# Earlier opening and denser feeding of 16-head attention stages, and zero products beside their first score maxima

## The chip, the cores and the metric

The kernel runs on one core of one Trainium2 chip. The metric is the device time of one execution in microseconds; it was taken three times. Engines are named as in the profile: PE is TensorE, the matrix engine; PEld is its load of weights; DVE is VectorE; ACT is ScalarE; POOL is GpSimd; SP is SyncE, which issues DMAs. A "granted clock" of 1.00 means that TensorE ran at its full clock, 0.50 at half.

## The reference

A sequence x of 2048 tokens with 128 features runs through fourteen residual sublayers, each on the layer norm of x. Three are softmax attention with 16 heads of 8 features, four are mixtures of 8 experts that are computed densely (Moe0 and Moe3). One of each, cut to what matters:

```python
# 16-head attention (causal and with rotary embedding in layer 0, plain in layer 2,
# with a spectral filter on q and k in layer 3)
att = einsum('bhqd,bhkd->bhqk', q, k) * (1.0 / sqrt(D))      # D = 8
att = softmax(where(causal, att, NEG_BIG), axis=-1)           # causal in layer 0 only
y = einsum('bhqk,bhkd->bhqd', att, v)
x = x + y.reshape(B, T, C) @ Wp.T + bp

# mixture of 8 experts, 128 -> 512 -> 128, every expert on every token
h = relu(einsum('td,edh->teh', xt, W1) + b1)
y = einsum('teh,ehd->ted', h, W2) + b2
x = x + einsum('ted,te->td', y, gate)                         # gate: top 2 of 8 (0 or 1 in Moe3)
```

## The kernel before

x stays in SBUF as 16 tiles of 128 tokens, in four blocks of 512 tokens (`NB` 4, `BW` 512). The list `STAGES` (L2199) names the fourteen stages in order, with their numbers: CumSum 0, Moe0 1, Causal 2, Moe0 3, Mamba 4, Mla 6, Ssm 7, Moe2 9, Attn2 10, Moe2 11, Hale 12, Moe3 13, Filtered 14, Moe3 15. Causal, Attn2 and Filtered are the 16-head stages and share the class `Attn16` (L641). Moe0 and Moe3 share the class `Moe` (L340); Moe2, which stands ahead of Attn2, is another class with a pace of its own.

**Handover between stages.** `Core.run` (L71) walks through a stage's `main`, which yields between pieces of work. At every `cur.pace`-th yield it advances the `feed` of the next stage by one step (L88). `feed` (L101) waits until the current stage is `roomy`, that is, has given back enough SBUF; then it opens the next stage, whose weight loads are issued there, and runs the early work of its blocks: `NB - own` of them, three for a 16-head stage, whose fourth is done within its own main. A block starts only when the current stage has finished that block of x, and no sooner than four steps after the one before it (`apart`), so three blocks want some 17 steps. When main has ended, what is left of the feed runs at once, one step behind another. Whatever is issued to an engine's queue runs there in that order. The stages with numbers below 12 are built in a block whose order of instructions a scheduler with a simulated timeline may change; from Hale on the order is nearly the one written. Matmuls that call `in_turn` keep their order in either.

**Moe.** `open` (L347) opens pools, loads small weights and calls `weights(e)` (L365) for two experts; the others are fetched two experts ahead within the first block. Each call loads raw f32 weights W1 and W2 into tiles from a pool `moe_s` of the whole stage (`self.two`, 2 or 1 buffers for each name) and splits each into a high and a low part in fp32r (`split`, L125 to L130, the copy on ACT and the difference on DVE). `main` (L469) goes over 4 blocks, 8 experts in a block and 4 quarters of the 512 hidden features in an expert, and yields after each quarter. A quarter is `first` (L425: three matmuls, L135 to L137, then the relu on ACT or DVE and the low part on POOL or DVE, L437 to L441) and, four quarters later, `second` (L443: L448 broadcasts the gate, three matmuls for W2, and after the fourth quarter L461 `m_t` on DVE and L462, the sum `m_acc` on POOL). After the last block four quarters drain, with a yield each, and `add_T` (L156) transposes `m_acc` and adds it to x. In the last block each expert that has been used for the last time shuts its weights' pool, for the last `SHUT` = 5 of the numbering (the order of experts is reversed in odd blocks, so the first five to be done); the stage is `roomy` after the fifth. `spare` is true unless the next stage is Mamba.

**Attn16.** The early work of a block is layer norm (L246 to L255), transposes (L262), the projection to v (L727), to k (`heads`, with L694 for the bias, L135 to L137 for the matmuls, rotary embedding at L702 to L704 in Causal, and the split), and four `slot`s that spread k over the four groups of heads (L715, copied by ACT at L717). `main` (L743) does the same for q's block 0 and runs `units` (L589): 16 units, a group of four heads by a block of queries. A unit has two passes. `pass_a` (L763) forms scores (L784), two heads at a time into a pair `ps_a` of PSUM banks, adds the causal mask on the diagonal (L787) and takes the maximum along the keys on DVE (L788); `set_max` (L800) turns the maxima (L810, L812) and a DMA (L814) writes them beside q, so that pass_b's matmuls subtract them. `pass_b` (L834) forms transposed scores (L868), takes their exponential on ACT (L874) and multiplies them with v (`av`, L847) into a PSUM tile of the tag "c"; each such step is followed by four matmuls with an all-zero weight into the same tile (L851, the "zero products": `zerob` is 128 rows by 32 columns of zeros, `wide` is 128 x 512 of ones, in bf16). The tile is taken at a unit's first AV (L841). pass_a runs ahead of pass_b by a whole unit and six pairs, so a stage begins with pass_a alone.

Of the kernel before, what the change touches and what calls it, by code (L numbers as in the profile page):

```python
# [12 lines left out]
F32 = mybir.dt.float32  # L13
# [7 lines left out]
P = 128  # L21
# [5 lines left out]
FF = 512  # L27
# [312 lines left out]
class Moe(Stage):  # L340
# [1 line left out]


    pairs, lns = False, 2
    pace = 2

    def open(self):  # L347
        c, ins, pre = self.c, self.c.ins, self.pre
        self.open_ln()
        self.lag, self.lnx, self.two = (4, 2, 2) if self.spare else (3,1,1)  # L350
        m = self.m = self.pool("moe_m")
        self.wr = c.load(m, "moe_wr", (P, E), ins[pre + "Wr"])
        self.br = c.load(m, "moe_br", (P, 4, E), ins[pre + "br"].unsqueeze(0).unsqueeze(0).to_broadcast([P, 4, E]))
        self.b1 = c.load(m, "moe_b1", (P, E, 4), ins[pre + "b1T"])
        self.b2 = c.load(m, "moe_b2", (P, E), ins[pre + "b2T"])
        self.sel = c.load(m, "moe_sel", (P, E, P), ins["sel24"], dtype=BF16)
        self.gTs, self.ngT = [m.tile([P, BW], BF16, name=f"g_gT{k}") for k in range(2)], 0
        for t in self.gTs:
            c.nc.gpsimd.memset(t, 0.0)
        self.st = self.pool("moe_s")  # L360
        self.w1, self.w2, self.L, self.gT, self.acc = {}, {}, {}, {}, {}
        for e in range(2):
            self.weights(e)

    def weights(self, e):  # L365
        if e in self.w1 or e >= E:
            return
        c, ins, pre = self.c, self.c.ins, self.pre
        wp = self.pool(f"moe_w{e}")
        for w, nm, sh, src in ((self.w1, "w1", (P, FF), ins[pre + "W1"][e]), (self.w2, "w2", (P, 4, P), ins[pre + "W2"][e].rearrange("(c p) d -> p c d", p=P))):  # L370
            raw = self.st.tile(list(sh), F32, name=f"moe_{nm}_raw", bufs=self.two)
            c.nc.sync.dma_start(raw, src)
            w[e] = tuple(wp.tile(list(sh), F32R, name=f"moe_{nm}{k}") for k in "hl")
            c.split(*w[e], raw, "a", "v")

    def logits(self, b):
        c, nc = self.c, self.c.nc
# [86 lines left out]
            self.shut(f"moe_w{e}")  # L464
            self.roomy = e == E - self.SHUT

    SHUT = 5

    def main(self):  # L469
        c = self.c  # L470
# [170 lines left out]
class Attn16(Attention):  # L641
# [45 lines left out]
    def heads(self, which, b):  # L687

        c, nc, wt = self.c, self.c.nc, self.wt
        pss = []  # L690
        for nm in (which, which + "r") if self.rope else (which,):
            pp = c.ps("b")
            if nm + "b" in wt:
                nc.tensor.matmul(pp, wt[nm + "b"], c.ones2, start=True, stop=False)  # L694
            c.mm3(pp, wt[nm], self.hl[b], start=nm + "b" not in wt)
            pss.append(pp)
        src = pss[0]
        if self.rope:
            s = slice(b * BW, (b + 1) * BW)
            cos, sin = [c.load(self.pre_k, "at_" + n, (P, BW), c.ins[n][:, s], bufs=1) for n in ("cosT", "sinT")]  # L700
            src = self.pre_k.tile([P, BW], F32, name="at_r0", bufs=1)
            nc.vector.tensor_tensor(src, pss[0], cos, ALU.mult)  # L702
            nc.vector.tensor_tensor(sin, pss[1], sin, ALU.mult)
            nc.gpsimd.tensor_tensor(src, src, sin, ALU.add)  # L704
        h, l = (self.pre_k.tile([P, BW], F32R, name=f"at_{which}{k}", bufs=1) for k in "hl")
        c.split(h, l, src, "a")
        return h, l

# [33 lines left out]

    def main(self):  # L743
        self.start()
        self.wk = self.pool("at_k", 2)
        self.qhl = self.heads("q", 0)
        self.prep(0, 0)
        self.banks()
        for b in range(self.have):
            add_bias(self.c, self.bo, b)  # L750
        self.roomy = True
        yield from self.units(self.scale)

    def prep(self, g, b):
        q = self.wk.tile([P, BW], F32R, name="at_q", bufs=self.NQ)
# [6 lines left out]
    def pass_a(self, u):  # L762

        c, nc = self.c, self.c.nc
        g, b, i0, i1 = u
        q, KT = self.qb[(g, b)], self.KT[g]
        mx = self.wk.tile([P, 4, 4, 4], F32, name="at_mx")
        nch = b + 1 if self.causal else 4  # L770
        steps = self.steps(u, nch)
        for n, (i, ch) in enumerate(steps):
            nk = P * (4 * b + i + 1) if self.causal else T
            w = min(BW, nk - ch * BW)
            diag = self.causal and ch == nch - 1
            self.need(ch + 1)
            left = [1, 0]
            while left:
                jj = self.pair if self.pair in left else left[0]
                left.remove(jj)  # L780
                pa = self.ps("a", (P, 2, BW))
                for k in range(2):
                    r = rows(2 * jj + k)
                    self.in_turn(nc.tensor.matmul(pa[:, k, :w], q[r, i * P : (i + 1) * P], KT[r, ch * BW : ch * BW + w], start=True, stop=True))  # L784
                if diag:
                    d = pa[:, :, w - P : w]
                    nc.vector.tensor_tensor(d, d, self.maskb.unsqueeze(1).to_broadcast([P, 2, P]), ALU.add)  # L787
                nc.vector.tensor_reduce(mx[:, i, 2 * jj : 2 * jj + 2, ch], pa[:, :, :w], AX.X, ALU.max)  # L788
                if n == len(steps) - 1 and not left:
                    self.due.append([2, u, self.set_max(lambda j: q[32 * j + 24 : 32 * j + 26], mx[:, :, :, 0:nch], i0, i1)])  # L790
                yield (n + 1 - len(left) / 2) / len(steps)
# [37 lines left out]
    def pass_b(self, u, scale):  # L829
# [7 lines left out]
        def av(kt, off, ps, half):  # L837


            if kt == i0 == g % 2 == half == 0:  # L840
                self.acc = c.ps("c")  # L841
            mid = (off + end) // 2
            s = slice(mid, end) if half else slice(off, mid)
            for j in (3, 2, 1, 0):
                h = 27 * (4 * (g // 2) + j) + 9 * (g % 2)
                start, stop = kt == i0 == g % 2 == half == 0, kt == nkt - 1 and g % 2 == half == 1
                self.in_turn(nc.tensor.matmul(self.acc[32 * j : 32 * j + 32, s], self.V[:, kt, h : h + 32], ps[j][:, s], start=start, stop=stop))  # L847
            z = s if kt == 0 or end < BW else slice(half * BW // 2, (half + 1) * BW // 2)
            for j in (3, 2, 1, 0):
                if not (kt == nkt - 1 and half):  # L850
                    self.in_turn(nc.tensor.matmul(self.acc[32 * j : 32 * j + 32, z], c.zerob, c.wide[:, z], start=False, stop=False))  # L851
            if kt == nkt - 1 and half:
                self.closed = u
            if kt == nkt - 1 and g % 2 == half == 1:
                self.u = self.wk.tile([P, BW], F32, name="at_u", tag="at_t", bufs=2)
                nc.scalar.copy(self.u, self.acc)  # L856
# [1509 lines left out]
```

## Times and profile before

| What | Value |
|---|---|
| Runs, us | 4895.5, 4889.99, 4889.27; median 4889.99 |
| Profiled execution, us | 4891.9 |
| Span of its trace, us | 4890.1 |
| Mean granted clock of TensorE | 0.917 |
| Instructions | 89638 |

The profiled execution is one more run, so sums made from its trace are held against 4891.9 and not against the median. Its busy times add up over stages with different limits, so windows of the trace are used beside the page. In the trace, Moe0(1) issues its last W2 matmul at 275.2 us and Causal its first scores at 320.0; Moe3(13) issues its last at 3922.1 and Filtered its first scores at 3950.8; Attn2's first maxima on their own begin at 2174.6. In the groups of the page, "out<-in (partitions x elements, type) xcount | busy, mean ns of one | idle time before, and what released it" is the order of the columns.

### The profile page before, as it was taken

What the parts mean: (1) busy time and instruction counts of PE and PEld (TensorE: products, weight loads), DVE (VectorE), ACT (ScalarE), POOL (GpSimd) and SP (SyncE); (2) the same over time, 40 slices, a digit from 0 to 9 for tenths busy, and PEclk for the clock granted to TensorE, in tenths of its full rate; (3) what the DMA queues carried; (4) which work ended last, traced back from release to release, by engine and by line L of the source; (5) the groups of instructions that cost most, each with busy time, mean ns of one, the idle gap of its engine ahead of it and who ended that gap; (6) DMA issues with size and microseconds to landing.
All of it is one profiled execution on the core that took longest, in us unless ns stands there. A gap on an engine that the chain in (4) does not pass through costs nothing.

```text
span 4890.1 us, 89638 instructions
## 1 busy us (share of the span) xinstructions
PE 4476.9 (92%) x36516; PEld 2519.0 (52%) x36534; DVE 3752.6 (77%) x5756; ACT 3058.1 (63%) x5527; POOL 938.1 (19%) x802
## 2 busy tenths in 40 slices
PE   6989999987799998899999998989988989999998
PEld 4744444654344443563444457666656744444466
DVE  7867895799766662779999957448777789999767
ACT  4634678865255555446888874345545648888876
POOL 4730000554000000320000013012215600000056
PEclk9966899997699999888999999889998969999999
DMA  1010000000000000000000000111221000000000
GB/s 51 6 44 6 4 2 4 22 1 16 17 14 14 18 14 8 4 1 2 2 2 2 2 4 1 39 51 48 52 51 37 4 12 2 2 2 2 2 20 7
DMA packets 68865, 72.84 MB, mean 15 GB/s; under 512 B 17505, under 2 KB 43991, under 8 KB 68326
## 3 DMA queue, kind: packets, MB, share of 16 engines
q1 hardware_dynamic: 68454, 67.12, 5.0%
q8 instruction: 288, 4.72, 0.4%
q14 instruction: 123, 1.01, 0.1%
HBM read 31.57 MB, written 1.05 MB: 7 GB/s over the span
## 4 chain that ended last, share of the span: by engine, by line
PE 60%; DVE 15%; ACT 3%; issue 2%; POOL 1%; DMA 0%; SPq 0%; POOLq 0%; ACTq 0%; DVEq 0%
PE ps_c L847 12%; PE ps_a L784 8%; PE ps_c L1438 5%; PE ps_b L1445 3%; PE ps_b L868 3%; PE ps_a L1411 3%; PE ps_c L851 2%; DVE at_mx L788 2%; PE ps_a L135 2%; PE ps_a L137 2%; PE ps_a L136 2%; DVE m_hl L441 1%; PE ps_b L135 1%; PE ps_b L2072 1%; PE ps_a L1677 1%
## 5 line engine op out<-in xcount | busy, mean ns | idle before, releaser
L874 ACT ACTIVATE at_P<-ps_b 128x512 f32<-128x512 f32 (+2 forms) x2688 | 1414.6, 581 | 328.1 <-PE ps_b L868 204.6
L788 DVE TENSOR_REDUCE at_mx<-ps_a 128x2 f32<-128x1024 f32 (+2 forms) x1344 | 1537.3, 1183 | 99.4 <-PE ps_b L868 59.5
L847 PE MATMUL ps_c<-at_P,at_V 128*32 128x256 f32 (+3 forms) x10752 | 863.1, 394 | 8.1 <-ACT at_u L856 7.6
L868 PE MATMUL ps_b<-at_q,at_KT 32*128 32x512 f32 (+2 forms) x2688 | 757.2, 497 | 6.9 <-DMA at_q<-at_mT 5.0
L784 PE MATMUL ps_a<-at_KT,at_q 32*128 32x512 f32 (+3 forms) x2688 | 698.3, 518 | 48.4 <-DVE at_mx L788 45.9
L784 PEld LDWEIGHTS ps_a<-at_KT,at_q 32*128 32x128 f32 x2688 | 266.5, 195 | 494.5 <-issue 329.8
L440 ACT ACTIVATE m_hh<-ps_a,moe_b 128x512 fp32r<-128x512 f32 x512 | 350.4, 690 | 193.2 <-DVE m_h L437 161.0
L441 POOL TENSOR_TENSOR m_hl<-m_h,m_hh 128x512 fp32r<-128x512 f32 x256 | 365.0, 1427 | 541.4 <-ACT m_hh L440 527.9
L1447 ACT ACTIVATE ml_P<-ps_b 128x512 f32<-128x512 f32 (+1 forms) x544 | 296.1, 572 | 240.7 <-PE ps_b L1445 233.9
L1412 DVE TENSOR_REDUCE ml_mx<-ps_a 128x2 f32<-128x1024 f32 x256 | 309.2, 1223 | 150.4 <-PE ps_a L1411 150.0
L847 PEld LDWEIGHTS ps_c<-at_P,at_V 128*32 128x32 f32 x10752 | 215.1, 109 | 356.3 <-issue 178.1
L851 PE MATMUL ps_c<-wide,zerob 128*32 128x256 bf16 x5184 | 389.1, 280 | 0.0
L252 POOL TENSOR_TENSOR ln_rs<-ln_ve,nhalf 128x4 f32<-128x4 f32 x56 | 59.4, 1062 | 1655.7 <-DVE ln_ve L250 1647.5
L868 PEld LDWEIGHTS ps_b<-at_q,at_KT 32*128 32x128 f32 x2688 | 325.3, 188 | 74.3 <-issue 44.7
L441 DVE TENSOR_TENSOR m_hl<-m_h,m_hh 128x512 fp32r<-128x512 f32 x256 | 258.4, 1010 | 78.0 <-ACT m_hh L440 77.3
L1438 PE MATMUL ps_c<-ml_P,ml_V 128*33 128x512 f32 (+3 forms) x1088 | 275.7, 585 | 5.3 <-ACT ml_P L1447 5.3
L439 ACT ACTIVATE m_h<-ps_a,moe_b 128x512 f32<-128x512 f32 x320 | 220.8, 690 | 71.5 <-DVE m_hl L441 33.7
L135 PE MATMUL ps_b<-m_hh,moe_w2h 128*128 128x512 f32 x512 | 222.6, 435 | 21.3 <-DVE m_t L461 18.2
L136 PE MATMUL ps_b<-m_hl,moe_w2h 128*128 128x512 f32 x512 | 214.1, 418 | 25.4 <-DVE m_hl L441 21.0
L135 PE MATMUL ps_a<-ln_h,moe_w1h 128*128 128x512 f32 x512 | 223.0, 437 | 14.4 <-ACT m_hh L440 14.2
L1445 PE MATMUL ps_b<-ml_pad,ml_KT 128*128 128x512 f32 (+1 forms) x544 | 210.8, 427 | 6.6 <-ACT ml_P L1447 5.4
L851 PEld LDWEIGHTS <-zerob 128*32 128x32 bf16 x5184 | 155.2, 100 | 112.3 <-issue 9.0
(642 smaller groups left out, 7869.0 us busy)
## 6 DMA issues: line engine op xcount, KB each, us to landing
hl_KS<-hl_pkh SPq DMA_DIRECT2D x160, 64.0 KB
moe_w_raw<-in_l0f_W SPq DMA_DIRECT2D x32, 256.0 KB
ml_pad<-ml_QT SPq DMA_DIRECT2D x32, 256.0 KB
moe_w_raw<-in_l3f_W SPq DMA_DIRECT2D x32, 256.0 KB
hl_KS<-hl_pkl SPq DMA_DIRECT2D x80, 64.0 KB
at_pad<-at_q SPq DMA_DIRECT2D x64, 64.0 KB
at_q<-at_mT SPq DMA_DIRECT2D x192, 4.0 KB
at_cosT<-in_cosT SPq DMA_DIRECT2D x8, 256.0 KB
```

What stands on the lines that cost most here:

```text
L135: nc.tensor.matmul(out, lh, rh, start=start, stop=False)
L136: nc.tensor.matmul(out, lh, rl, start=False, stop=False)
L440: nc.scalar.activation(hh, ph, AF.Relu, bias=bias)
L441: (nc.gpsimd if f in ((0, 2) if self.spare else MS) else nc.vector).tensor_tensor(hl, h, hh.bitcast(F32), ALU.subtract)
L784: self.in_turn(nc.tensor.matmul(pa[:, k, :w], q[r, i * P : (i + 1) * P], KT[r, ch * BW : ch * BW + w], start=True, stop=True))
L788: nc.vector.tensor_reduce(mx[:, i, 2 * jj : 2 * jj + 2, ch], pa[:, :, :w], AX.X, ALU.max)
L847: self.in_turn(nc.tensor.matmul(self.acc[32 * j : 32 * j + 32, s], self.V[:, kt, h : h + 32], ps[j][:, s], start=start, stop=stop))
L851: self.in_turn(nc.tensor.matmul(self.acc[32 * j : 32 * j + 32, z], c.zerob, c.wide[:, z], start=False, stop=False))
L868: self.in_turn(nc.tensor.matmul(pbs[k][:, off:end], KT[r, kt * P : (kt + 1) * P], q[r, off:end], start=True, stop=not diag))
L874: nc.scalar.activation(p[:, off:end], pbs[k][:, off:end], AF.Exp, scale=scale)
L1438: nc.tensor.matmul(acc[64 * j : 64 * j + m, s], v, ps[j][:, s], start=(kt == 0), stop=(kt == NT - 1))
L1445: nc.tensor.matmul(pb[:, s], self.KT[2 * g + j][:, kt * P : (kt + 1) * P], qb[:, j, s], start=True, stop=True)
```

## The change

Three things change together.

1. **Feeding.** In `Moe`, `pace` becomes 1 where `spare` is true and stays 2 otherwise, so Causal and Filtered are fed at every yield and Mamba at every second. `SHUT` goes from 5 to 3: only three experts give their weights back early, and the next stage opens after the third expert of the last block instead of the fifth. This holds for every `Moe`, that before Mamba included.
2. **Memory.** The raw weights no longer come from one pool for the stage; each call of `weights(e)` opens `moe_s` above its own expert's weights and shuts it at its end, one buffer a name. The split q of a block (`at_qh`, `at_ql`) comes from a pool that main opens, not from the one that the opening of the stage takes.
3. **Zero products.** `Attn16.main` takes the "c" tile before its units. After each maximum in `pass_a`, as long as no AV has begun, `filled` issues eight matmuls of `zerob` with all 512 columns of `wide` into that tile (two rounds of the four groups of 32 columns). The first AV then takes a tile of its own and ends this. The program holds 17 such fills in Causal, 41 in Attn2 and 41 in Filtered, 792 matmuls; the counts of all other instructions stay the same.

```diff
--- before.py
+++ after.py
@@ -342,7 +342,7 @@
 
 
     pairs, lns = False, 2
-    pace = 2
+    pace = property(lambda self: 1 if self.spare else 2)
 
     def open(self):
         c, ins, pre = self.c, self.c.ins, self.pre
@@ -357,7 +357,6 @@
         self.gTs, self.ngT = [m.tile([P, BW], BF16, name=f"g_gT{k}") for k in range(2)], 0
         for t in self.gTs:
             c.nc.gpsimd.memset(t, 0.0)
-        self.st = self.pool("moe_s")
         self.w1, self.w2, self.L, self.gT, self.acc = {}, {}, {}, {}, {}
         for e in range(2):
             self.weights(e)
@@ -367,11 +366,14 @@
             return
         c, ins, pre = self.c, self.c.ins, self.pre
         wp = self.pool(f"moe_w{e}")
-        for w, nm, sh, src in ((self.w1, "w1", (P, FF), ins[pre + "W1"][e]), (self.w2, "w2", (P, 4, P), ins[pre + "W2"][e].rearrange("(c p) d -> p c d", p=P))):
-            raw = self.st.tile(list(sh), F32, name=f"moe_{nm}_raw", bufs=self.two)
+        for w, nm, sh in ((self.w1, "w1", (P, FF)), (self.w2, "w2", (P, 4, P))):
+            w[e] = tuple(wp.tile(list(sh), F32R, name=f"moe_{nm}{k}") for k in "hl")
+        st = self.pool("moe_s")
+        for w, nm, src in ((self.w1, "w1", ins[pre + "W1"][e]), (self.w2, "w2", ins[pre + "W2"][e].rearrange("(c p) d -> p c d", p=P))):
+            raw = st.tile(list(w[e][0].shape), F32, name=f"moe_{nm}_raw")
             c.nc.sync.dma_start(raw, src)
-            w[e] = tuple(wp.tile(list(sh), F32R, name=f"moe_{nm}{k}") for k in "hl")
             c.split(*w[e], raw, "a", "v")
+        self.shut("moe_s")
 
     def logits(self, b):
         c, nc = self.c, self.c.nc
@@ -464,7 +466,7 @@
             self.shut(f"moe_w{e}")
             self.roomy = e == E - self.SHUT
 
-    SHUT = 5
+    SHUT = 3
 
     def main(self):
         c = self.c
@@ -702,7 +704,8 @@
             nc.vector.tensor_tensor(src, pss[0], cos, ALU.mult)
             nc.vector.tensor_tensor(sin, pss[1], sin, ALU.mult)
             nc.gpsimd.tensor_tensor(src, src, sin, ALU.add)
-        h, l = (self.pre_k.tile([P, BW], F32R, name=f"at_{which}{k}", bufs=1) for k in "hl")
+        pool = self.wk if which == "q" else self.pre_k
+        h, l = (pool.tile([P, BW], F32R, name=f"at_{which}{k}", bufs=1) for k in "hl")
         c.split(h, l, src, "a")
         return h, l
 
@@ -742,14 +745,24 @@
 
     def main(self):
         self.start()
+        c = self.c
         self.wk = self.pool("at_k", 2)
         self.qhl = self.heads("q", 0)
         self.prep(0, 0)
         self.banks()
         for b in range(self.have):
-            add_bias(self.c, self.bo, b)
+            add_bias(c, self.bo, b)
         self.roomy = True
+        self.fill = c.ps("c")
         yield from self.units(self.scale)
+
+    def filled(self):
+
+        if self.fill is None:
+            return
+        for _ in range(2):
+            for j in (3, 2, 1, 0):
+                self.in_turn(self.c.nc.tensor.matmul(self.fill[32 * j : 32 * j + 32, :], self.c.zerob, self.c.wide, start=True, stop=True))
 
     def prep(self, g, b):
         q = self.wk.tile([P, BW], F32R, name="at_q", bufs=self.NQ)
@@ -786,6 +799,7 @@
                     d = pa[:, :, w - P : w]
                     nc.vector.tensor_tensor(d, d, self.maskb.unsqueeze(1).to_broadcast([P, 2, P]), ALU.add)
                 nc.vector.tensor_reduce(mx[:, i, 2 * jj : 2 * jj + 2, ch], pa[:, :, :w], AX.X, ALU.max)
+                self.filled()
                 if n == len(steps) - 1 and not left:
                     self.due.append([2, u, self.set_max(lambda j: q[32 * j + 24 : 32 * j + 26], mx[:, :, :, 0:nch], i0, i1)])
                 yield (n + 1 - len(left) / 2) / len(steps)
@@ -838,7 +852,7 @@
 
 
             if kt == i0 == g % 2 == half == 0:
-                self.acc = c.ps("c")
+                self.acc, self.fill = c.ps("c"), None
             mid = (off + end) // 2
             s = slice(mid, end) if half else slice(off, mid)
             for j in (3, 2, 1, 0):
```

## Prediction

> **What bounds the kernel now.** I read the page's busy shares and slices first, then the chain by engine, then the costliest groups, and last a table of windows around the three places where a Moe hands over to a 16-head stage, with PE's timeline inside them.
>
> ```profile
> PE 4476.9 (92%) x36516; PEld 2519.0 (52%) x36534; DVE 3752.6 (77%) x5756; ACT 3058.1 (63%) x5527; POOL 938.1 (19%) x802
> ...
> PEclk9966899997699999888999999889998969999999
> ...
> PE 60%; DVE 15%; ACT 3%; issue 2%; POOL 1%; DMA 0%; SPq 0%; POOLq 0%; ACTq 0%; DVEq 0%
> ...
> L788 DVE TENSOR_REDUCE at_mx<-ps_a 128x2 f32<-128x1024 f32 (+2 forms) x1344 | 1537.3, 1183 | 99.4 <-PE ps_b L868 59.5
> ```
>
> TensorE is busy 92% of the span and is 60% of the chain; VectorE's 15% is next, with L788, the maxima of the scores, ahead. The clock row shows where TensorE is slow rather than idle: slices three and four (about 245 to 490 us) stand at 6. The windows say why. Columns: stretch in us, its length, busy time of PE, PEld, DVE, ACT, POOL (instructions), granted clock, DMA share, GB/s.
>
> ```profile
> 235.80:275.60 39.80, 37.09 (x155) 27.79 (x154) 31.18 (x48) 22.94 (x38) 31.92 (x28) 0.96 0.11 34
> 275.60:320.00 44.40, 32.97 (x95) 18.54 (x94) 21.32 (x43) 14.03 (x23) 10.45 (x9) 0.53 0.27 80
> 320.00:342.20 22.20, 14.74 (x55) 7.58 (x55) 19.26 (x38) 4.79 (x8) 1.26 (x1) 0.50 0.07 24
> 342.20:442.00 99.80, 96.55 (x734) 45.07 (x734) 64.19 (x114) 39.32 (x92) 2.29 (x2) 0.52 0.02 7
> 259.50:270.00 10.50, 8.12 (x36) 5.77 (x35) 10.50 (x22) 4.67 (x8) 7.54 (x6) 1.00 0.02 7
> ```
>
> The first row is the end of Moe0(1), PE nearly full at full clock. From its last second matmul (275.6) to Causal's first scores (320.0) lie 44.4 us at clock 0.53: the feed's leftovers, projections of blocks 1 and 2, run one behind the other. Then come the first maxima (no AV yet), where DVE leads, and 100 us in which PE is busy 96.55 us at half clock. The same for the later sites: Attn2's first maxima and the ramp after them, then Filtered's prologue, maxima and ramp:
>
> ```profile
> 2187.80:2224.80 37.00, 25.85 (x75) 9.99 (x73) 36.56 (x36) 3.58 (x6) 0.00 (x0) 0.50 0.00 1
> 2224.80:2234.10 9.30, 9.30 (x59) 4.12 (x60) 4.91 (x4) 5.54 (x10) 0.00 (x0) 0.50 0.00 1
> 3922.50:3950.80 28.30, 22.99 (x69) 13.14 (x69) 12.80 (x28) 12.23 (x22) 6.26 (x6) 0.58 0.13 39
> 3950.80:3998.30 47.50, 34.52 (x99) 13.89 (x98) 45.33 (x43) 4.84 (x9) 0.00 (x0) 0.50 0.00 0
> 3998.30:4005.60 7.30, 7.30 (x42) 3.17 (x42) 3.68 (x3) 4.45 (x8) 0.00 (x0) 0.50 0.01 4
> ```
>
> In the maxima DVE is busy 36.56 of 37.00 and 45.33 of 47.50, so PE's half clock costs nothing there. The bill comes after: 9.30 and 7.30 us with PE full at half clock until the clock returns.
>
> **1. The Moe opens the next stage two experts sooner and feeds at every yield.** A projection block wants about 17 feed steps for three blocks. Before, 9 yields and 4 of draining at pace 2 give 6 or 7 steps; now 17 and 4 at pace 1 give 21, so all three blocks are issued inside the Moe (the instruction order of the two programs shows this: blocks 1 and 2 stand ahead of the last m_acc transposes).
>
> Causal. Of the 32.97 us that PE is busy in the 44.4, 1.1 are the m_acc transposes and some 4.3 q's heads; the other 27.6, at half clock, are blocks 1 and 2, so they put 13.8 us at full clock into the Moe's end. DVE's 21.32 there are about 7 us for each block and as much for q. In the last row above (259.5 to 270.0, where block 0 is fed) DVE is full at 10.50 and PE is at 8.12; over the whole tail PE has 37.1 + 13.8 = 51 and DVE 31.2 + 14 = 45, so PE bounds and the tail grows by about 13.8. What stays of the 44.4 us: the wait for m_acc and its transposes (0.4 to 278.2 + 1.1, about 4 us) and q's heads. That chain shows in the timeline (start, us, engine, line):
>
> ```profile
> 307.92 0.79 PE L694 MATMUL ps_b<-ones,at_bq 2*128 2x512 f32 x1
> ...
> 319.99 0.48 PE L784 MATMUL ps_a<-at_KT,at_q 32*128 32x128 f32 x3
> ```
>
> 320.0 - 307.9 = 12.1 us, with rival block work between; alone it is perhaps 9. So 44.4 becomes 13.8 + 4 + 9 = 26.8, a gain of some **17.5** (12 if the DVE-bound row holds throughout the longer tail, 20 if projections hide in the 2.7 us that PE was idle).
>
> Filtered. The 28.3 us row has two blocks of plain (no rope) projection at half clock. Of PE's 22.99, 0.66 are m_acc's and some 3.4 q's; the other 19 move into the Moe at full clock, about 10 us; what stays is 3 us of m_acc wait (2.97 before L156 in the timeline) and 5 to 6.4 us from q's first matmul (3944.34) to first scores (3950.75). 28.3 - (10 + 3.6 + 6.4) = **8** (5 to 10). This Moe has no next Moe to load for; its successor's four raw loads now stand on SP behind Filtered's small loads, and their splits (four on DVE, 0.69 us each, 2.8 us in all) fall among Filtered's first maxima where DVE is the bound: +2.8 at worst. I take +1 and keep -7 for the site.
>
> Moe0(3), ahead of Mamba, keeps pace 2 but opens Mamba two experts sooner; Mamba is in the region whose order a scheduler sets. Its instruction counts are unchanged. No row prices a reshuffle; the nearest is the first site, two experts' lead for up to 17 us when projections had been late. I take 0, bounds -8 to +8.
>
> **2. Raw weights get a pool for each expert.** The same loads and splits, but one raw buffer pair an expert instead of a rotating pair for the stage. An expert has 25 matmuls, 5.8 us of PE, and its load is issued two experts ahead; the 0.96 clock with PE 37.09 of 39.80 says nothing waits for weights in the steady part. Cost 0; if cover is gone in the first block, where weights are loaded, one late load an expert would be a microsecond or two, six experts, two Moes: kept as +8 in the stage bound above. SP's queue: Causal's block-3 cos/sin load stands behind the next Moe's expert-1 load, which waits for space; it is needed hundreds of us later, so 0. Moving at_qh and at_ql to another pool adds no instruction.
>
> **3. Zero products with the first maxima.** 17 fills in Causal, 41 in Attn2, 41 in Filtered, eight matmuls each (32 columns by 512, four column groups): 792 matmuls. A single group of four at 256 columns is this row (and its time in the ramp):
>
> ```profile
> 2231.07 0.44 PE L851 MATMUL ps_c<-wide,zerob 128*32 128x256 bf16 x4
> ...
> 2235.07 0.29 PE L851 MATMUL ps_c<-wide,zerob 128*32 128x256 bf16 x4
> ```
>
> 0.44 us at half clock, 0.29 at full, with pitches of 0.37 and 0.23. Eight at 512 columns are four such groups' work in two: 0.74 to 0.88 at half clock (I take 0.85), 0.43 to 0.50 at full. A step then wants, of PE, 0.79 + 0.85 = 1.64 at half clock and 0.49 + 0.45 = 0.94 at full, against the maximum's pitch of 1.13 on DVE. So everything turns on whether the clock rises. In this trace it does not follow PE's busy time: 342 to 442 is PE-full at 0.52. It rose in the ramp soon after 2228, when full-height products (L847, L851) joined the 32-row scores. A fill is exactly such work, half of a 1.64 us step, so I expect the clock to rise within one or two of its 3.4 us records. Cost of a cold start: 3 to 4 steps x 0.51 = about 1.5 to 2 in each stage. Queued behind a fill on PE are the next scores, and DVE waits for those alone; there are two ps_a tiles ahead.
>
> Gain: Attn2's 9.3 us ramp at half clock would be 4.6 at full if the clock holds through the 1.72 us wait for the DMA that writes the maxima; Filtered's 7.3 would be 5. Attn2 net **-1** (-5 to +4); Filtered +1.5 - 1.5 = 0. Causal: fills against a window with PE 14.74 of 22.2: at half clock 14.74 + 14.5 = 29.2, 7 over; at full about 15, hidden. +1.5, and then the prize, the 99.8 us at half clock. Held throughout, DVE's 64.2 plus starts would set it, about 68, so -31; lost at the first DMA wait, 0. Causal's narrow first units have few full-height products, and PE full at 0.52 shows they do not lift the clock alone; whether they hold it once up is not shown. I take **-5**.
>
> The Trainium skill, page "TensorE: Matmul & The Clock Gate", section "Part 1: The HAM clock gate", says that one busy window of about 3.4 us opens the full clock and one idle window closes it. The row of 342.2 to 442.0 (PE busy 96.55 of 99.80, clock 0.52) differs: busy is not enough here. By the page's rule a short DMA wait would not close it, and the sum would end near -45; by the row it ends near my number.
>
> **Sum.** Causal -17.5 + 1.5 - 5 = -21; Attn2 -1; Filtered -7; the rest 0, and 1 for waits unseen: -28. The profiled execution is 4891.9 (span 4890.1), 1.9 over the median of 4890.0, so 4864 against it and 4862 against the median; I give **4864**.
>
> **Rivals.** *Clock held*: Causal's first 100 us run at full clock: 25 sooner than taken, 4839, and with Attn2's ramp halved about 4834. For: a zero product follows each AV already. Against: 100 us at PE-full and 0.52. *Prologue given back*: DVE, full in the fed row, bounds the whole of the tail; PE's order puts projections ahead of second matmuls that m_t and m_acc wait for. The 25 us of moves give 5 to 10, and the clock nothing: 4880 to 4893. For: 10.50 of 10.50. *Fills at half clock, slower*: the place is the first maxima of Attn2 and Filtered; if the clock does not rise, a step is 1.64 for 1.13, 82 x 0.51 = 42, and Causal 7 to 14: about +52 - 25 = +27, 4919. It decides from a step pitch above 1.44 (25 us over 82 steps = 0.31 over 1.13). Against: a fill is full-height work. *Not what it says*: the sooner opening only reorders and waits on PE's own queue, within 0.2%: 4890.
>
> **Chances.** Forecast case (4850 to 4878) 0.50; held 0.15; given back 0.15; no effect 0.05; fills at half clock 0.15. Two tenths may be left out: the low end takes in half of held, the high end given back and part of slower: 4834 to 4903. 0.2% is 10 us, what a measurement of this kernel can tell. Faster (under 4880): forecast, held and 0.02 of given back, 0.67. Slower (over 4900): fills at half clock and 0.02 of no effect, should a term at nothing go bad, 0.17. Within: the rest, 0.16.
>
> **What would show it.** Right: first scores of Causal 15 to 20 us sooner, of Filtered 6 to 10; blocks 1 and 2 ahead of the last L156; maxima pitch of 1.13 unchanged, and the clock at 1.0 a few us into Attn2's and Filtered's first unit, with the fills' groups near 0.5 us. Wrong: L788 waiting for scores, at a pitch near 1.6 with the clock at 0.50 throughout (the slower rival); Moe tails longer by 20 or more with DVE full (given back); windows of Causal's first units at 0.9 (held). A change of more than 8 us in the span of Mamba or of the Moes' first blocks would break the sum at the term I put at nothing.

## The result and the profile after

The changed kernel takes 4946.66 us in the median of four runs (4941.72 to 4967.05), the kernel before 4889.63 (4880.12 to 4895.5): a ratio of 1.0126, 95% interval 1.0092 to 1.016. It is **slower by 57 us** (1.3%), where 26 less were forecast. The profiled execution took 4941.89, close to the fastest of the four; its span is 4940.1, 50.0 us over the span of before. The lines of the page that answer to those shown of before:

```profile
PE 4535.9 (92%) x37308; PEld 2518.1 (51%) x37326; DVE 3748.8 (76%) x5756; ACT 3061.4 (62%) x5527; POOL 934.3 (19%) x802
...
PEclk9966897898599999899999999789998999999999
...
PE 71%; DVE 19%; ACT 4%; issue 3%; POOL 1%; DMA 1%; SPq 0%; POOLq 0%; ACTq 0%; DVEq 0%
...
L801 DVE TENSOR_REDUCE at_mx<-ps_a 128x2 f32<-128x1024 f32 (+2 forms) x1344 | 1541.6, 1184 | 120.4 <-PE ps_b L882 73.6
```

All engines are about as busy as before, PE by 59 us more, with 792 matmuls added; its share of the chain is 71% instead of 60, and L801 (L788 before) waits 21 us more. The clock row says where to look: slices seven and eight (741 to 988 us) read 7 8 instead of 9 9, in Causal's last block and the Moe after it.

A better finder is the update of x that ends every block of a stage, the same 96 instructions of VectorE in both traces. Their time after, less their time before, is flat where nothing happened and steps where time was lost (+) or won (-). The main steps of all kernels, in us; the experiments e1 to e14 are told below, and "site 3" is Moe3(13)'s last block and Filtered's first together:

| kernel | start | Moe0(1), last block | Causal block 1 | 2 | 3 | 4 | Attn2 block 1 | site 3 |
|---|---|---|---|---|---|---|---|---|
| after | +3.2 | +31.5 | -17.6 | -4.5 | +1.1 | +35.7 | +4.2 | +2.7 |
| e1 fills alone | -0.4 | +0.7 | +9.2 | +2.6 | -1.2 | +27.1 | +29.1 | +27.2 |
| e2 feed alone | +3.1 | +31.2 | -35.3 | +7.1 | +9.0 | +1.6 | +0.6 | -0.7 |
| e3 memory alone | +3.3 | -1.2 | -7.7 | -4.4 | +16.7 | +1.6 | +0.5 | -3.3 |
| e4 open sooner | +3.1 | +7.8 | -10.0 | -2.2 | +1.1 | +0.1 | +0.7 | -4.7 |
| e5 narrow, data | -0.2 | +1.9 | +9.7 | +7.3 | 0.0 | 0.0 | +27.1 | +27.8 |
| e6 full, zeros | +0.1 | -0.6 | +8.7 | -4.1 | +9.2 | +25.1 | +0.9 | +26.6 |
| e7 full, data | -0.3 | +1.8 | +4.3 | -5.4 | +21.8 | +0.3 | +3.7 | +26.7 |
| e8 after, in line | +2.2 | +30.4 | -35.3 | -6.3 | +0.7 | +0.3 | +28.2 | +23.7 |
| e9 before, in line | +0.4 | +2.0 | +0.7 | -7.4 | +0.7 | +20.8 | +0.3 | -1.8 |
| e10 sooner, in line | +2.7 | +8.2 | -21.8 | -4.5 | +1.9 | +0.1 | +0.8 | -4.8 |
| e11 feed, in line | +3.4 | +31.2 | -38.0 | -3.1 | +0.3 | +0.3 | +3.2 | -2.2 |
| e12 half fills | +0.8 | +1.9 | +4.7 | -2.3 | +16.7 | +1.6 | +8.0 | +10.7 |
| e13 feed, slots later | +2.5 | +22.8 | -36.2 | -3.9 | +0.7 | +0.3 | +0.4 | -3.3 |
| e14 sooner, slots later | +3.5 | +8.0 | -22.7 | -0.7 | +0.4 | +0.2 | +0.4 | -6.6 |

Each row is one profiled execution and prices that execution, not the median: those of e1, e6 and e8 are the slowest of their runs, that of e10 is the fastest. Smaller steps are left out; the largest of them in after is -6.9 over Moe3(13)'s first three blocks. Of after, three places want an explanation: the Moe's end and Causal's first block together (+13.9, where -21 was forecast), Causal's fourth block (+35.7, forecast 0), Attn2 and site 3 (+6.9, forecast -8).

**The first place.** Windows of after: the Moe's end in two parts (its last second matmul ends at 311.4), the prologue to the first scores (324.1), the first maxima, and the units up to 428.6. The columns are those of the windows in the prediction.

```profile
238.30:279.00 40.70, 34.52 (x135) 24.77 (x133) 31.17 (x51) 21.02 (x34) 27.18 (x25) 0.87 0.11 33
279.00:311.40 32.40, 26.02 (x88) 16.51 (x87) 12.22 (x20) 13.97 (x23) 9.33 (x7) 0.84 0.15 49
311.40:324.10 12.70, 6.92 (x20) 3.54 (x20) 9.09 (x22) 3.06 (x5) 5.58 (x6) 0.68 0.36 106
324.10:345.00 20.90, 20.90 (x111) 8.42 (x114) 13.44 (x24) 1.96 (x4) 2.10 (x2) 0.50 0.08 26
345.00:428.60 83.60, 81.99 (x616) 35.04 (x608) 50.40 (x88) 30.26 (x72) 1.27 (x1) 0.50 0.03 8
```

The prologue has shrunk from 44.4 us to 12.7, as forecast. But the Moe's end is 32.6 us longer (311.4 - 275.6, less the 3.2 lost at the start), with PE idle for 12.6 of its 73.1 us and the clock at 0.84 to 0.87. PE's waits in it (engine, what waited, on what: us in all, times, longest):

```profile
PE ps_b L718 <- ACT at_kh L129: 9.9, 3, 4.2
PE ps_a L135 <- ACT m_hh L442: 0.9, 1, 0.9
```

L718 is the first slot of a block: k has been projected, and VectorE, GpSimd and ScalarE are still at the rotary embedding and the split. The Moe's next second matmuls are queued behind it. Around each of these three waits the clock falls, to 0.50 in 264.7 to 271.6, 285.2 to 288.6 and 298.9 to 305.7, which stretches the work as well: PE is busy for 60.5 us where the prediction had 51. Then, in the fourth window above, PE is busy without a gap at half clock: the fills.

**The second place.** Causal's fourth block, in windows of 20 us that run side by side; before first:

```profile
726.30:746.30 20.00, 19.93 (x272) 9.24 (x274) 18.92 (x22) 15.73 (x35) 0.00 (x0) 1.00 0.01 2
746.30:766.30 20.00, 20.00 (x272) 8.84 (x268) 19.70 (x23) 17.52 (x34) 0.00 (x0) 1.00 0.01 2
```

After:

```profile
740.00:760.00 20.00, 18.10 (x170) 7.33 (x169) 12.14 (x16) 9.08 (x21) 0.00 (x0) 0.57 0.01 2
760.00:780.00 20.00, 20.00 (x263) 8.58 (x263) 18.79 (x21) 17.74 (x33) 0.00 (x0) 1.00 0.01 2
840.00:880.00 40.00, 40.00 (x350) 15.15 (x346) 0.00 (x0) 23.26 (x48) 0.00 (x0) 0.61 0.02 8
```

PE does 170 matmuls instead of 272 in the first of them, busy all but 1.9 us, at 0.57. That 1.9 us is where it starts; the timeline of PE in after:

```profile
742.07 0.40 PE L824 MATMUL ps_b<-identr,at_mhl 128*8 128x128 f32 x4 [1.90 <-DVE at_mhl L819]
```

and of VectorE, in after and then, at the same place, in before:

```profile
738.03 2.36 DVE L801 TENSOR_REDUCE at_mx<-ps_a 128x2 f32<-128x1024 f32 x2
740.30 0.21 DVE L816 TENSOR_REDUCE at_m<-at_mx 128x16 f32<-128x64 f32 x1
740.54 0.18 DVE L818 CAST at_mhl<-at_m 128x16 fp32r<-128x16 f32 x1
740.63 1.22 DVE L801 TENSOR_REDUCE at_mx<-ps_a 128x2 f32<-128x1024 f32 x1
741.76 0.17 DVE L819 TENSOR_TENSOR at_mhl<-at_m,at_mhl 128x16 fp32r<-128x16 f32 x1
```

```profile
725.62 0.22 DVE L802 TENSOR_REDUCE at_m<-at_mx 128x16 f32<-128x64 f32 x1
725.88 0.17 DVE L804 CAST at_mhl<-at_m 128x16 fp32r<-128x16 f32 x1
726.09 0.18 DVE L805 TENSOR_TENSOR at_mhl<-at_m,at_mhl 128x16 fp32r<-128x16 f32 x1
```

A maximum of 1.22 us of the next unit stands between the three small operations of `set_max`. In before they follow each other at this place. Nothing in the diff touches them; they lie in the part whose order the scheduler sets. After has three stretches at half clock in this block: 742.6 to 759.7 and 790.4 to 814.3, each behind such a wait (1.90 and 1.86 us), and 848.4 to 892.8, the longest. The last row of after above holds most of it, with PE busy 40.00 of 40.00 us: no wait leads to that one.

### The profile page after: what moved, and what is told of

The parts are those of the page before. It is cut to its first block, busy times and chain, and to the rows that moved or that the text cites. A ratio compares the mean times of both kernels' runs of the same rounds, so it can differ in the third digit from the quotient of the medians.

```text
span 4940.1 us, 91210 instructions
## 1 busy us (share of the span) xinstructions
PE 4535.9 (92%) x37308; PEld 2518.1 (51%) x37326; DVE 3748.8 (76%) x5756; ACT 3061.4 (62%) x5527; POOL 934.3 (19%) x802
## 3 DMA queue, kind: packets, MB, share of 16 engines
HBM read 31.57 MB, written 1.05 MB: 7 GB/s over the span
## 4 chain that ended last, share of the span: by engine, by line
PE 71%; DVE 19%; ACT 4%; issue 3%; POOL 1%; DMA 1%; SPq 0%; POOLq 0%; ACTq 0%; DVEq 0%
PE ps_c L861 15%; PE ps_a L797 10%; PE ps_c L1452 5%; DVE at_mx L801 4%; PE ps_b L882 4%; PE ps_b L1459 3%; PE ps_c L865 3%; PE ps_a L1425 3%; PE ps_a L135 2%; PE ps_a L136 2%; PE ps_a L137 2%; PE ps_b L135 2%; DVE m_hl L443 2%; PE ps_b L136 2%; PE ps_b L137 2%
## 5 line engine op out<-in xcount | busy, mean ns | idle before, releaser
L801 DVE TENSOR_REDUCE at_mx<-ps_a 128x2 f32<-128x1024 f32 (+2 forms) x1344 | 1541.6, 1184 | 120.4 <-PE ps_b L882 73.6
L861 PE MATMUL ps_c<-at_P,at_V 128*32 128x256 f32 (+3 forms) x10752 | 880.7, 401 | 7.8 <-ACT at_u L870 7.3
L797 PE MATMUL ps_a<-at_KT,at_q 32*128 32x512 f32 (+3 forms) x2688 | 685.1, 507 | 25.4 <-DVE at_mx L801 19.2
L136 PE MATMUL ps_b<-m_hl,moe_w2h 128*128 128x512 f32 x512 | 215.8, 421 | 29.5 <-DVE m_hl L443 23.7
L865 PEld LDWEIGHTS <-zerob 128*32 128x32 bf16 x5184 | 157.6, 102 | 117.4 <-issue 16.7
```

Of the source, the lines that this page charges most:

```text
L136: nc.tensor.matmul(out, lh, rl, start=False, stop=False)
```

## The experiments

My first theory had separate causes: waits at the slots eat the prologue, fills run at half clock, and the order on VectorE costs Causal its clock. The rival was that the fills are the whole loss. "Fills" are the zero products of the first maxima.

**e1, the fills alone** on the kernel before. The edit is cut to its calls; `filled` is that of the change.

```diff
+        self.fill = self.c.ps("c")                # Attn16.main, ahead of the units
+                self.filled()                     # pass_a, after each maximum
-                self.acc = c.ps("c")
+                self.acc, self.fill = c.ps("c"), None
```

> The kernel before with the zero products of the first maxima alone (no earlier opening, no denser feed, raw weights as before). Theory 1, several separate causes: the fills cost about 13 us in Causal's first units, where the clock stayed at 0.50 under them in the changed kernel, some 4 us in Attn2 and 7 us in Filtered, where they raise the clock but lose it at the wait for the maxima's DMA; the 36 us lost in Causal's last block come from another cause (a maximum placed ahead of the unit's own small reductions on VectorE) and are absent here: about +24 us, 4914. Rival, the fills are the whole loss: +50 us or more, 4940.

4955.07 us (4931.14 to 4989.35), ratio 1.0137 (1.0105 to 1.017). The total fits the rival. The traced execution is the slowest of the six (4989.35), so its steps come to more than the 67 us between the medians. The table says more: +29.1 in Attn2, +27.2 in Filtered, +9.2 in Causal's first block, and +27.1 in Causal's fourth, where no maximum stands between set_max's operations, as in before. So such a loss does not need the order that I had made its cause. Attn2's first maxima and the ramp behind them:

```profile
2217.30:2291.40 74.10, 73.40 (x418) 20.92 (x414) 51.41 (x52) 4.75 (x8) 2.28 (x2) 0.50 0.00 1
2291.40:2302.00 10.60, 10.55 (x70) 3.54 (x70) 4.66 (x4) 5.39 (x10) 0.00 (x0) 0.50 0.01 3
```

Fills with 128 rows, PE full, and the clock stays at 0.50 for 74 us. The same loop in PE's timeline, here:

```profile
2250.11 1.05 PE L761 MATMUL ps_c<-wide,zerob 128*32 128x512 bf16 x8
2251.09 0.79 PE L793 MATMUL ps_a<-at_KT,at_q 32*128 32x512 f32 x2
2251.81 1.04 PE L761 MATMUL ps_c<-wide,zerob 128*32 128x512 bf16 x8
```

and in after, where the clock did rise:

```profile
2250.99 0.61 PE L765 MATMUL ps_c<-wide,zerob 128*32 128x512 bf16 x8
2251.70 0.49 PE L797 MATMUL ps_a<-at_KT,at_q 32*128 32x512 f32 x2
2252.12 0.61 PE L765 MATMUL ps_c<-wide,zerob 128*32 128x512 bf16 x8
```

A steady step is 1.70 us at half clock, PE its bound, and 1.13 at full, VectorE its bound.

**e2, the feed alone**: the changed kernel with `self.fill = None` in main.

> The changed kernel without any zero product (earlier opening, pace 1, raw pool for each expert stay). Theory 1: Causal's prologue gains nothing, since each k slot waits on TensorE for the rotary chain with the Moe's second matmuls queued behind it (first scores within 3 us of before plus 3 us lost at the start); Filtered's first scores come 4 to 5 us sooner; Moe3(13) is some 7 us shorter; no loss in Causal's last block: -10 to 0 us, 4880 to 4890. Rival, the fills are the whole loss and the feed brings what was predicted: -25 us, 4865. Rival, the feed itself is what costs: +20 us or more, 4910 and over.

4898.64 us, 1.0019 (1.0008 to 1.0029): 11 us over before: neither the theory's 4880 to 4890 nor what either rival expected. The prologue's waits are as in after (L718: 4.2, 2.8 and 2.8 us; first scores at 322.4 against 320.0 before), and Causal's blocks 2 and 3 lose 16.1 us to half clock.

**e3, the memory alone**: after without fills, `pace = 2`, `SHUT = 5`.

> The kernel before with only the pools changed: raw weights from a pool opened for each expert, split q from main's pool; SHUT 5, pace 2, no zero products. Theory 1: the 3.3 us that the changed kernel loses ahead of the first update of x are here (one raw buffer a name instead of two), and so are the 7 us that Moe3(13) gains: 4884 to 4890. Rival, memory is free: 4890 with the first update of x at 51.0 us as before.

4898.74 us (4884.14 to 4925.39), 1.0027 (1.0008 to 1.0045), over the theory's 4884 to 4890; the profiled run 4891.4 in span. The 3.3 us at the start are here, as in every kernel with the new pools (2.2 to 3.5) and in none without (0.8 at most). So are 6.7 won over Moe3(13)'s first three blocks, but e6 and e7, with the raw weights as before, won 7.8 and 7.7 there: that the pools won them is not shown. Causal's third block ran partly at half clock (+16.7) in this execution.

**e4, opening sooner**: as e3 with `SHUT = 3`.

> As the feed alone, but with pace 2 in every Moe: the next stage opens after the third expert of the last block and gets a step at every second yield; no zero products. Theory 1: with more Moe work between a block's k heads and its slots the waits of 3 to 4 us at each block's first slot are gone or shorter, so Causal's first scores come 5 to 10 us sooner than in the feed alone: 4875 to 4885. Rival, the projections' cost in the Moe's tail is the work itself (VectorE full) and not the waits: equal to the feed alone within 3 us.

4881.5 us, 0.9991 (0.998 to 1.0002), 17 us below the feed alone; that much the theory had. Its reason is only half met: the Moe's end comes 23.4 us sooner than in the feed alone, but blocks 1 and 2 then follow it, with a wait of 9.4 us for at_kh, and Causal's first scores (320.9) are only 1.5 us sooner, as the rival had it. Of the 22.6 us between the two profiled executions, 17.2 lie in Causal's blocks 2 and 3, which lost 16.1 us in that of the feed alone and won 1.1 here.

**e5, e6, e7: what lifts the clock?** The fills alone, with other operands: narrow groups of x's values; a whole array of zeros; a whole array of x's values. The products are discarded in all.

```diff
-  matmul(self.fill[32 * j : 32 * j + 32, :], self.c.zerob, self.c.wide, ...)           # four groups, twice
+  matmul(self.fill[32 * j : 32 * j + 32, :], self.some[:, 32 * j : 32 * j + 32], self.some, ...)   # e5
+  matmul(self.fill, self.some[:, 0:P], self.c.wide, ...)     # e6, some = 0, twice
+  matmul(self.fill, self.some[:, 0:P], self.some, ...)       # e7, twice
```

> As the fills alone (the kernel before and fills at the first maxima), but the weights and the moving rows of each fill are values of x in bf16 instead of zeros and ones; same shapes (four 32-column groups, 512 columns, twice), the product is discarded, and one copy on VectorE in each of the three stages is added. Theory, the monitor behind the clock does not count products of zeros: the clock is 1.00 within 10 us of the first fill in Attn2 and Filtered, a step of those maxima takes 1.13 us, and the run is within 10 us of before, 4880 to 4900. Rival, what counts is only the shape: half clock through the maxima of at least one of the stages as in the fills alone (0.50 for 80 us), a step of 1.7 to 1.9 us, 4930 to 4960.

> As the fills alone, but each fill is two matmuls of a 128 x 128 weight of zeros with 512 columns instead of eight of 128 x 32 (one small memset in each stage is added). Theory, zeros are not counted: half clock through the maxima of Attn2 and Filtered, 4930 to 4960. Rival, the four 32-column groups count for less than a whole array: the clock rises within 10 us, 4880 to 4900.

> As the fills alone, but each fill is two matmuls of a 128 x 128 weight with 512 columns, both values of x in bf16. Theory, zeros are not counted, and rival, narrow groups are not counted: both expect the clock at 1.00 within 10 us of the first fill in Attn2 and Filtered, a step of 1.13 us and 4875 to 4900. If the clock still stays at 0.50, neither the zeros nor the narrow groups are why, and work at half clock cannot lift the clock by itself.

e5 4954.09 us, 1.0134 (1.0098 to 1.0171); e6 4929.27, 1.0085 (1.0055 to 1.0116); e7 4946.14, 1.0112 (1.0089 to 1.0134). e5 came out as its rival had it. For e6 and e7 theory and rival each had the two stages alike, and they were not: in Filtered all three kernels stayed at half clock (+26.6 to +27.8); in Attn2 e5 did (+27.1), e6 and e7 rose (+0.9, +3.7). So neither the zeros nor the narrow groups alone keep the clock down; whether a whole array makes the rise more likely is not settled by two kernels. What the table does show is **two prices and nothing between**: over the six traced kernels with full-length fills, 1 to 4 us in Attn2 where the clock rose (after, e6, e7), 27 to 29 where it did not (e1, e5, e8).

**e8, VectorE's order kept**: the changed kernel, with the maxima, the mask and set_max's three operations held in the order written. The edit is cut to its helper, which wraps these five operations.

```diff
+    def in_line(self, i):
+        if self.pre:
+            self.c.tc.stamp_issue_order_token(i.ins, self.pre + "dve")
```

> The changed kernel with one thing more: on VectorE the maxima, the mask and the three small operations of set_max keep the order in which they are written, in all 16-head stages. Theory: the two waits of 1.9 us for at_mhl in Causal's last block, after each of which the clock fell to 0.50 for 17 to 24 us, are gone, and with them most of the 36 us lost there: 4905 to 4925. Rival, the clock there falls by chance and the order has no part in it: 4935 to 4965.

4906.3 us over eight runs (4885.12 to 4928.81), 1.0037 (1.0018 to 1.0056): 40 us faster than after, with no run as slow as after's fastest. The theory's 4905 to 4925 is met. The waits for at_mhl are gone, Causal's fourth block is at +0.3, its first at -35.3. In this execution, the slowest of the eight, Attn2 and Filtered both ran their fills at half clock; the mean granted clock of the eight runs goes from 0.921 in the slowest to 0.933 in the fastest. In Causal the clock rose under the same fills that stood at 0.50 in after; its first maxima here:

```profile
320.70:341.60 20.90, 19.09 (x155) 8.45 (x158) 16.73 (x34) 4.79 (x8) 2.18 (x2) 0.87 0.08 26
```

**e9, the order kept on the kernel before**, nothing else.

> The kernel before with VectorE's maxima, mask and set_max kept in the order written in the 16-head stages, nothing else. The kernel before has a maximum among set_max's operations in only two of the eight units of Causal's last two blocks and lost nothing visible there, so theory: the order alone is worth little here, 4878 to 4890; first scores and Moe tails as before. Rival, the order is a gain of its own in any kernel: 4850 to 4870.

4890.95 us, 0.9995 (0.998 to 1.001): no gain by itself, as the theory had it. And its fourth block shows +20.8, at half clock from 812 to 863 us, without a wait for at_mhl. Keeping the order takes one trigger away, not the fall itself. How often it triggers shows in Causal's third block: where the order is free, TensorE waits 1.05 us for at_mhl there; in e2, e3, e6 and e12 the clock fell at that wait (+9.0 to +16.7), in before, after, e1, e4 and e5 it did not.

**e10, opening sooner with the order kept** (e4 and e8's edit), and **e11, the feed alone with the order kept** (e2 and e8's edit).

> Opening two experts sooner with pace 2 in every Moe, no zero products, and the order on VectorE kept. Theory: the gain of the earlier opening (in its own run first scores in Filtered 10 us sooner for the Moe's 5, and 7 us in Moe3(13)) and no chance losses in Causal: 4865 to 4880, the fastest version so far. Rival: the same as the earlier opening without the order, 4878 to 4885.

> The changed kernel without zero products and with the order on VectorE kept; beside the changed kernel with the order kept and the zero products (4906), it prices the zero products with that cause of noise away. Theory, the fills cost 27 us for each of Attn2 and Filtered in which the clock stays at half, and little else: 4870 to 4890. Rival, the fills are free once the order is right: 4900 to 4910.

e10: 4872.1 us, 0.9963 (0.995 to 0.9976), 9 below e4. e11: 4880.84, 0.9987 (0.9972 to 1.0001), 18 below e2. Both lie where their theories had them. Against e8 (4906.3) e11 prices the fills at 25 us with the order out of the way. That is the theory's number for one of the two stages at half clock; that runs of e8 differ in which stage falls is likely from their clocks, but only one of them was traced.

**e12, half the fills**: one round of four matmuls.

> As the fills alone, with one round of four matmuls for each pair instead of two. Theory, what a fill costs is its time at half clock where the clock does not rise: a step then takes 0.72 + 0.52 = 1.24 us instead of 1.75, against 1.13 of VectorE, so Attn2 and Filtered lose 5 us each instead of 27, and Causal 4 to 5 instead of 9: 4895 to 4915. Rival, the loss comes from the fills' being there (the queue, the PSUM tile), not from their length: 4935 to 4960.

4936.53 us, 1.0096 (1.0083 to 1.0109): the total is the rival's, the price nearer the theory's. Attn2 lost 8.0 and site 3 10.7 (forecast 5 each, 27 to 29 with full fills), and Causal's first block 4.7; 16.7 more are the third block, where the clock fell at the wait for at_mhl. The step, from PE's timeline:

```profile
2229.65 0.62 PE L761 MATMUL ps_c<-wide,zerob 128*32 128x512 bf16 x4
2230.20 0.79 PE L793 MATMUL ps_a<-at_KT,at_q 32*128 32x512 f32 x2
2230.93 0.62 PE L761 MATMUL ps_c<-wide,zerob 128*32 128x512 bf16 x4
```

1.28 us, 0.15 over VectorE's 1.13, for 41 steps: 6 of the 8.

**e13 and e14, slots later**: e11 and e10 with two empty feed steps between a block's k heads and its first slot.

```diff
         hl = self.heads("k", b)
         yield
+        yield
+        yield
         for g in range(4):
```

> The feed at every yield without zero products and with the order on VectorE kept, and two empty feed steps more between a block's k heads and its first slot. In the program's order 21 Moe matmul rows then stand between them for block 0 (3 without), still none for blocks 1 and 2. Theory, the tail of the Moe loses its time where TensorE waits for the rotary chain at the first slot with the Moe's matmuls queued behind: the wait of 4.2 us at block 0 is gone, the two of 2.8 us stay, and the Moe's end in front of Causal comes 3 to 5 us sooner than the 31 us it is late there. Rival, the work of the projections itself fills the tail: no change there within 1 us.

> The opening two experts sooner at pace 2 without zero products, order kept (4872, the fastest so far), and the same two empty feed steps. Theory: at pace 2 block 0's chain is covered already (27 rows between) and the empty steps only push blocks 1 and 2 behind the Moe's end: 0 to 6 us slower than without them, 4870 to 4880. Rival: fewer waits in the tail here too, 4860 to 4868.

e13: 4865.82 us, 0.9956 (0.9942 to 0.9969). e14: 4866.81, 0.995 (0.993 to 0.997). Both beat both kernels. e14 fits its rival, 5 us under e10 where the theory had it no better, but the intervals of the two overlap. e13's waits in the Moe's end, against 9.9 us for L718 above:

```profile
PE ps_b L135 <- DVE at_r L704: 1.4, 1, 1.4
...
PE ps_b L718 <- ACT at_kh L129: 0.5, 1, 0.5
```

Of the three waits 0.5 us remain, where the theory had only the first gone. Against e11, the same kernel without the empty steps, the Moe's end is 8.4 us shorter and Causal's first scores come 9.5 us sooner (314.5 for 324.0) with the same work. So the waits were the cause of these 8 to 9 us. Here first scores are 5.5 us sooner than before although the start lost 2.5: a gain of 8, half of the 17.5 that was forecast.

## Where the prediction was wrong

The sum was -28 and the profiled execution is at +50, 78 us apart. Of these, 35 lie in Causal's prologue and first block (+13.9 for -21), 36 in its fourth block (+35.7 for 0), 15 in Attn2 and site 3 (+6.9 for -8) and 3 at the start; the other steps, Moe3(13)'s -6.9 first among them, take the rest back. So two steps failed in what was traced, the overlap of the feed with the Moe and the term "the rest 0". A third, the clock's rise under the fills, held there and failed in e1, e5 and e8.

**The fills, "I expect the clock to rise within one or two of its 3.4 us records".** In the traced execution of after it did, in both Attn2 and Filtered, 7 us after the fills began. It is not a rule: e1 ran 74 us of fills at 0.50 with PE full, and without fills the kernel is 25 us faster in the median (e11 against e8). I had read the rise in the ramp of before as the work of full-height products; e5 to e7 show that full height, full width and real values do not lift it reliably. For e1 the slower rival had the mechanism, its place and nearly its price: 82 steps of 0.51 were 42 us for Attn2 and Filtered, and e1 measured 56 (29.1 + 27.2; a steady step of 1.70 for 1.64, above the 1.44 from which that rival was to decide, and more in the steps that share TensorE with projections). Its chance of 0.15 was too low: nothing in the trace of before spoke for the loop at full clock. Where the clock rose, the fills cost 4.2 in Attn2 and 5 in site 3 (Filtered's first block -13.2 for -18.2 in e11), where I had put a cold start at 1.5 to 2.

**The ramp, "would be 4.6 at full if the clock holds through the 1.72 us wait".** It did not hold. Even where the fills had run at full clock, the clock fell at the wait for the DMA, and the ramp took 10.4 us (9.30 before):

```profile
2227.40:2271.60 44.20, 40.32 (x381) 13.35 (x377) 42.95 (x43) 4.17 (x7) 0.00 (x0) 1.00 0.00 1
2271.60:2282.00 10.40, 10.40 (x70) 3.42 (x70) 4.51 (x4) 5.25 (x10) 0.00 (x0) 0.51 0.01 3
```

So the best case of the fills that was traced is a small loss: they speed up a stretch that VectorE bounds, and the speed is gone when PE is the bound.

**Causal, "-5" for the held clock and "+1.5" for the fills.** The clock stayed at 0.50 from 315.9 to 428.6. Causal's first block is 17.7 us slower than without fills (-17.6 against -35.3 in e2). That is not the fills' price alone, though 17 fills of 1.04 us would make it: e8 has the same fills and stands at -35.3 too. At half clock throughout, as in before, the fills cost 9.2 (e1); the rest of the 17.7 is clock that rose now and then in e2 and not in after. The block moves with the clock even without a change of the feed: e3, with the feed of before, won 7.7 in it.

**The prologue, -17.5: "PE bounds and the tail grows by about 13.8".** It grew by 32.6. I had added busy times and left out that TensorE works in order: at a step for each quarter, the slot stands right behind its k heads in the queue, and the rotary chain lasts longer than what lies between. With the clock that fell around these waits that gave back the whole gain: first scores 4.1 us later than before, 3.2 of them from the start. Taking the waits away returned 8.4 of the 18.8 us over the forecast (e13 against e11); the other 10 stay open, with the clock still at 0.90 there in e13. The rival "prologue given back" was right in what came of the prologue, and near in its second reason (the order on PE); VectorE, its first reason, is busy for 43.4 of the 73.1 us. For Filtered, without rotary embedding, part of the gain came: first scores 4.7 us sooner (3990.9 less the 44.8 of delay carried in, against 3950.8), forecast 8.

**"The rest 0", within 8.** Causal's fourth block alone lost 35.7. I had looked for a changed order in Mamba and not on VectorE within Causal, although the same scheduler sets it. Two of after's three stretches at half clock there follow a 1.9 us wait for at_mhl, and with the order kept the kernel is 40 us faster. The third and longest, 44 us, follows no wait, and e1, e6 and e9 fell in this block without one: what starts these falls is open. Raw weights were not free: +3.3 us at the start.

**The clock rule.** The Trainium skill, page "TensorE: Matmul & The Clock Gate", section "Part 1: The HAM clock gate", has the full clock open after one busy window of about 3.4 us. e1's window with PE busy 73.40 of 74.10 us at 0.50 speaks against it, as the row of before did, if busy is what the profile counts as busy. That a short DMA wait would not close the clock, as the prediction read that section, did not hold either: in after a wait of 1.43 us for the maxima's DMA ends at 2271.6, and the clock is 0.51 in the 10.4 us behind it. For a held clock the prediction's own terms give -53 (its 4839), not the -45 that it names by that rule.

In medians, taken one after the other: the feed and the memory with the order kept are worth -8 us (e11, interval touching no change), the fills on top +25 (e8 over e11), the free order on top of both +40 (after over e8). That they come to +57 follows from the way they are taken and confirms nothing by itself. The +40 is what the order is worth in this kernel: on before it is worth nothing (e9), without the fills 18 (e2 over e11).

**Left open.** What the clock's monitor counts. Before, it rose in 7 to 10 us of the ramps and for one 3.4 us record only in 100 us of Causal's first units; identical loops ran at 0.50 or 1.00. Which of the two a stage gets was not controlled by any edit here.

## What to carry to other kernels

Adding idle work to keep TensorE's clock up must be priced at half clock first: if it makes TensorE the bound there, the loop can stay at half clock for its whole length, and the price is the full difference of the two steps. When early work is fed into another stage, count the wait between dependent steps on an in-order engine, not the sum of busy times: two empty steps won 15 us in the median (e13 against e11). In a part whose order a scheduler sets, compare the order of every engine, VectorE's small operations included, since two waits of 1.9 us on TensorE were followed here by 17 and 24 us at half clock.

## What was not expected of the hardware

The granted clock showed two steady states for the same instructions: the loop of scores and fills ran at 0.50 with PE busy 99% and at 1.00 with PE busy 91%, each for 40 us and more. Kernels whose stages can land in either scatter: the fills alone ran between 4931 and 4989 us, the kernel before, on the same chip, between 4878 and 4900.
